# Layer 0's division and projection taken strip by strip, and attention scores with 64 keys at a time

## The chip, the cores and the metric

The kernel runs on one core of a Trainium2 chip. Its time is the device time of one execution in microseconds (us), the median of several runs. The core has five engines [...]: TensorE (PE, with its weight loads shown apart as PEld), VectorE (DVE), ScalarE (ACT), GpSimd (POOL) and SyncE (SP, which here issues DMA transfers). [...]

## The reference, cut to what matters

An image of 256 channels and 64 x 64 pixels goes through two layers. All numbers are fp32.

```python
# layer 0: linear attention over boxes, 8 heads of 32 channels
q, k = sigmoid(Wq @ x), sigmoid(Wk @ x)          # x after a group norm
v = v / norm(v)                                  # per head, v = Wv @ x
for w in (1, 2, 4):                              # boxes of 64, 32 and 16 pixels
    wk, wkv = box_sum(k), box_sum(k v^T)         # around each pixel
    attn = (q @ wkv) / (q @ wk + 1e-06)
    outs.append(attn)
x = x + Wout @ concat(outs) + bout
# layer 1: layer norm, softmax attention over 4096 tokens (8 heads of 32),
t = t + attention(layer_norm(t))
# then a mixture of 8 experts, two for each token
t = t + experts(layer_norm(t))
```

## The kernel before

**Order of pixels.** The image is cut into eight vertical strips `ix`, each 64 rows by 8 columns, 512 pixels. A strip has eight cells of 8 x 8 pixels. A block of 128 keys is two cells. `NB = 4` blocks make a strip.

**Layer 0, the two halves.** The outer loop `for g in range(KC)` does four heads at a time, 128 channels. For each half `prepare` projects keys, values and queries, makes sums over cells (`ssum`), and gets the denominators `den` of all three boxes and eight strips by matmuls into one PSUM bank. From it comes `rec`, 128 x 512: the row for strip `ix`, box `w` and head is `D * (ix % 4) + 4 * (NCH // 4 * w + ix // 4) + head`. Line 529 adds 1e-6, line 530 takes the reciprocal.

**Layer 0, the windows.** `attend` then goes through the three boxes, `for w in (2, 1, 0)`. A box reaches r = 1, 2 or 4 cells to each side (`REACH = (4, 2, 1)`). For r = 2 and r = 4 it first makes a vertical pass over four row bands `b` (L612 scores, L631 sums of whole cells, L643 values), copied into `raw` by ACT (L656), and then a pass over the strips `ix` (L681 scores, L697 values). For r = 1 there is the pass over strips alone. The result of a strip is added to `raw` by DVE (L707), or for r = 1 copied there by ACT (L709).

A *step* packs jobs of up to 512 queries. It has four score matmuls per job, one for each head, each with 32 rows of contraction; `masked` then multiplies each of the four heads' scores with a mask into `sm`. Heads 0 and 2 go by DVE from PSUM. Head 1, and in every other step head 3, are copied by ACT (L557) and multiplied by GpSimd (L561); head 3 else goes by DVE. The value matmuls of a step are put behind by two steps (`behind`, `tick`), so the order on TensorE is: scores of step n, values of step n - 2. Scores have six PSUM banks (`ps_sc`), sums have two (`ps_acc`).

**Layer 0, division and projection.** When a window is done, all steps in flight are flushed and two kinds of *chores* are listed. `division` takes two strips: a matmul (L721) with a constant of zeros and ones spreads the rows of `rec` over the 32 channels of each head, and DVE multiplies `raw` by it (L728). `projection` of a strip is eight 128 x 128 by 256 matmuls (L734), whose sums DVE adds to `t` (L738). `step_done` pops one chore after each step of the next window; the chores of the last window run at the end, with nothing beside them.

**Layer 1.** For each chunk of 512 queries `qc` and each half `g` there is a *group* of 32 steps, one for each block of 128 keys. A step has four score matmuls with 128 keys (L994) into two pairs of banks (`ps_two`, three pairs in all), two exponentials by ACT (L1004, one for each pair of heads), the value matmuls of the step before (L962), and sums of the exponentials by DVE in 30 of the 32 steps (L1011). The exponentials lie in a ring of four (`pe`). At the end of a group one matmul per head sums the last exponentials (`ps_den<-pe`), and a step later another adds the sums of DVE (`ps_den<-total`).

[...] 32 rows of contraction, and as many columns as it has keys or channels. In the profile 32*128 stands for 32 rows and 128 columns. Every fp32 matmul shows as two records.

Of the kernel before, what the change touches and what calls it, by code (L numbers as in the profile page):

```python
# [22 lines left out]
F32 = mybir.dt.float32  # L23
# [7 lines left out]
P = 128  # L31
C = 256
KC = C // P
N = 4096
NT = N // P
CH = 512
NCH = N // CH
IMG = 64
SW = 8
BH = 16  # L40
NB = IMG // BH
CELL = SW * SW
D = 32
GRP = 8
REACH = (4, 2, 1)
NW = len(REACH)
# [14 lines left out]
    "c": {"group": P, "xmask": 3 * SW, "ymask": SW * sum(_MCELLS), "ycut": 2 * SW},  # L61
    "k": {"sums": NCH // 4 * NW * D, "spread": NCH // 4 * NW * P, "before8": CH, "sides": NB * (SW + IMG + 1)},
    "m": {"rank": NE, "iota": P, "before": P, "ones": P, "number": 1, "high": 2 * NT, "spare": NU, "unit": NS + NE, "least": 2 * NE},
}
_AT, _W = {}, 0
# [6 lines left out]
def constants():  # L72
# [3 lines left out]
    out = np.zeros((P, _W), np.float32)  # L76
    p = np.arange(P)
# [9 lines left out]


    ns = range(NCH // 4 * NW)
    col = np.arange(D)[None, :]  # L90
    out[:, _AT["sums"]] = np.concatenate([col == 4 * n + p[:, None] // D for n in ns], 1)
    col = np.arange(P)[None, :]
    out[:, _AT["spread"]] = np.concatenate([p[:, None] % D == 4 * n + col // D for n in ns], 1)

# [20 lines left out]
def tile_conv_attn_hybrid(ctx: ExitStack, tc: tile.TileContext, a: dict, out: bass.AP):  # L115
    nc = tc.nc
# [26 lines left out]
    def tok(i):  # L143
        return slice(P * i, P * (i + 1))

    def chunk(i):
        return slice(CH * i, CH * (i + 1))
# [29 lines left out]
    def flush():  # L177
        while chains:
            tick()
# [9 lines left out]
    with ExitStack() as phase:  # L189
# [8 lines left out]

        big = phase.enter_context(tc.tile_pool(name="c_big", bufs=1))

        def weights(g):

            gs = slice(P * g, P * (g + 1))
            w3 = big.tile([P, KC, 3, P], F32, tag="w3", name="w3")
            for n, name in enumerate(("wqT", "wkT", "wvT")):
                nc.sync.dma_start(w3[:, :, n, :], a[name][:, gs].rearrange("(k p) o -> p k o", p=P))
            woT = big.tile([P, NW, C], F32, tag="woT", name="woT")
            nc.sync.dma_start(
                woT, a["woutT"].rearrange("(w g p) o -> p w g o", g=KC, p=P)[:, :, g, :]
            )  # L210
            return w3, woT

        with (
# [23 lines left out]
            for i in range(4):  # L237
                for k in range(KC):
                    at = slice(i * N // 4, (i + 1) * N // 4)
                    (nc.sync if k else nc.scalar).dma_start(x[:, k, at], xr[:, k, at])  # L240
            first = weights(0)
            ck = constants_of("k", wts)
# [63 lines left out]

        def prepare(g, prep, ps):


            bank, _ = banks(ps)  # L310
            two_banks = lambda: ps.tile([P, 2, CH], F32, tag="two", name="ps_two", bufs=3)
            w3, woT = weights(g) if g else first

# [215 lines left out]
            nc.vector.tensor_scalar_add(rec, den, 1e-6)  # L529
            nc.vector.reciprocal(rec, rec)  # L530
            return qk, v, ssum, rec, woT
# [3 lines left out]

        def finish(strip):

            while any(ix <= strip for ix, _ in chores):
                chores.pop(0)[1]()

        def step_done():
            tick()
            if chores:
                chores.pop(0)[1]()

        turns = [0]

        def masked(work, scs, used, pieces):


            turns[0] += 1
            sms = []
            for h, sc in enumerate(scs):
                sm = work.tile([P, CH], F32, tag="sm", name="sm", bufs=12)
                src, engine = sc, nc.vector
                if h == 1 or h == 3 and turns[0] % 2:
                    nc.scalar.copy(sm[:, :used], sc[:, :used])  # L557
                    src, engine = sm, nc.gpsimd
                for at, n, mk in pieces:
                    to, of = (z[:, at : at + n].rearrange("p (m n) -> p m n", n=mk.shape[-1]) for z in (sm, src))  # L560
                    engine.tensor_mul(to, of, mk.unsqueeze(1).to_broadcast(list(to.shape)))  # L561
                sms.append(sm)
            return sms
# [20 lines left out]
        def attend(g, work, ps, qk, v, ssum, rec, woT):  # L584
# [5 lines left out]
            raw = big.tile([P, NCH, CH], F32, tag="raw", name="raw")  # L590
            for w in (2, 1, 0):
                r = REACH[w]

                for b in (1, 2, 0, 3) if r > 1 else ():
# [8 lines left out]
                    for step in steps:  # L605
# [19 lines left out]
                        def use(places=places, sms=sms, accs=accs, begun=begun, b=b, last=step is steps[-1], raw=raw, r=r):  # L625
# [25 lines left out]
                            if last:  # L651

                                finish(NCH)
                                for u in range(2):
                                    q0 = P * b + CELL * u
                                    nc.scalar.copy(  # L656
                                        raw[:, :, q0 : q0 + CELL], accs[u].rearrange("p (i n) -> p i n", n=CELL)
                                    )
# [4 lines left out]
                for ix in range(NCH):  # L663
# [12 lines left out]
                    for step in steps:  # L676
                        scs = [score() for _ in range(4)]
                        at, places = 0, []
                        for n, i, c0, c1, *mk in step:
                            for h in range(4):  # L680
                                nc.tensor.matmul(  # L681
                                    scs[h][:, at : at + n],
                                    kT[hs[h], tok(i)],
                                    qT[hs[h], CH * ix + CELL * c0 : CH * ix + CELL * c1],
                                    start=True,
                                    stop=True,
                                    skip_group_check=True,
                                )
                            places.append((at, n, i, c0, c1, *mk))
                            at += n  # L690
                        sms = masked(work, scs, at, joined((p[0], p[1], *p[-2:]) for p in places))
                        step_done()

                        def use(places=places, sms=sms, acc=acc, begun=begun, ix=ix, last=step is steps[-1], raw=raw, r=r):
                            for at, n, i, c0, c1, *_ in places:
# [10 lines left out]
                            if last and r > 1:  # L706
                                nc.vector.tensor_add(raw[:, ix, :], acc, raw[:, ix, :])  # L707
                            elif last:
                                nc.scalar.copy(raw[:, ix, :], acc)  # L709

                        behind(lambda: None, use)

                flush()

                def division(ix, raw=raw, w=w):

                    for i, by in ((ix, score()), (ix + 1, score())):
                        at, n = slice(D * (i % 4), D * (i % 4 + 1)), NCH // 4 * w + i // 4  # L720
                        nc.tensor.matmul(  # L721
                            by,
                            ck["spread"][at, P * n : P * (n + 1)],
                            rec[at, :],
                            start=True,
                            stop=True,
                        )
                        nc.vector.tensor_mul(raw[:, i, :], raw[:, i, :], by)  # L728

                def projection(ix, raw=raw, w=w):  # L730
                    for b in range(0, NB, 2):
                        po = score().rearrange("p (i o) -> p i o", o=C)
                        for i in range(2):
                            nc.tensor.matmul(  # L734
                                po[:, i, :], raw[:, ix, tok(b + i)], woT[:, w, :], start=True, stop=True
                            )
                        to = t[:, NB * ix + b : NB * ix + b + 2, :C]
                        nc.vector.tensor_add(to, po, to)  # L738

                for ix in range(0, NCH + 2, 2):  # L740
                    if ix < NCH:
                        chores.append((ix, lambda ix=ix, f=division: f(ix)))
                    for i in (ix - 2, ix - 1) if ix else ():
                        chores.append((i, lambda i=i, f=projection: f(i)))
            finish(NCH)

        for g in range(KC):
            with tc.tile_pool(name="c_prep", bufs=1) as prep, psum("c_ps1", 2) as ps:
                of = prepare(g, prep, ps)
            with tc.tile_pool(name="c_work", bufs=1) as work, psum("c_ps2", 1) as ps:  # L750
                attend(g, work, ps, *of)
# [33 lines left out]
    with ExitStack() as phase:  # L785
# [163 lines left out]
        with tc.If(tame > 0) as branch:  # L949
            with (  # L950
# [33 lines left out]
                for qc in range(NCH):  # L984
                    for g in range(KC):
# [4 lines left out]
                        for i in range(NT):  # L990
                            sc = [two_banks() for _ in range(2)]
                            for hd in range(4):
                                hs = slice(D * hd, D * (hd + 1))
                                nc.tensor.matmul(  # L994
                                    sc[hd // 2][:, hd % 2, :],
                                    qk[hs, 1, g, tok(i)],
                                    qk[hs, 0, g, chunk(qc)],
                                    start=True,
                                    stop=True,
                                )  # L1000
                            pe = work.tile([P, 4, CH], F32, name="pe", bufs=4)
# [545 lines left out]
```

## Time and profile before

| | us |
|---|---|
| median of 3 runs | 2913.63 (2911.81 to 2914.61) |
| the profiled execution | 2911.62 |
| its span | 2909.8 |
| layer 0, half 0: windows | 141.6 to 526.2 |
| layer 0, half 1: windows | 642.1 to 1029.5 |
| layer 1: attention | 1147 to 2315 |
| layer 1: experts, output | 2315 to 2909.8 |

The profile is one execution. A matmul's record begins when it is issued and its end is modelled, so busy time of PE overlaps with its waits; the distance between the starts of two batches is what they really take. "Idle before" names what ended an engine's idle time. Times in the timeline are from the start of the span.

### The profile page before, as it was taken

The page shows a single profiled execution, that of the slowest core. Times are in us where ns is not written, and L with a number is a line of the kernel's source. Part 1 is how long each engine was busy: PE and PEld are TensorE (multiplying, and loading weights), DVE is VectorE, ACT ScalarE, POOL GpSimd, SP SyncE. Part 2 cuts the span into 40 slices and gives each one's busy share as a digit, 9 for nine tenths or more (in the row PEclk, how much of TensorE's full clock was granted, in tenths as well). Part 3 has the DMA queues.
Part 4 walks back from the last instruction along what each step waited for, and adds up shares of the span by engine and source line. Part 5 has one row for each costly group of instructions (what it writes and reads, how often), then busy time and mean ns, then how long its engine had stood idle before and what let it go on. Part 6 is the DMA issues. An engine that isn't in the chain of part 4 may idle for free. (4 is left out here: it accounts for less than half of the span.)

```text
span 2909.8 us, 62928 instructions
## 1 busy us (share of the span) xinstructions
PE 2769.2 (95%) x26286; PEld 1329.9 (46%) x26286; DVE 2082.3 (72%) x3009; ACT 1529.6 (53%) x2134; POOL 712.4 (24%) x808
## 2 busy tenths in 40 slices
PE   6899999989999988999999999999999969999996
PEld 5466442735644254222222222222222248888884
DVE  6776777577676886999999999999999941111113
ACT  3242323124233312888888888888888642222222
POOL 1085858109485711000000000000000012222220
PEclk9999999999999999999999999999999969999997
DMA  5000000000000000000000000000000056565665
GB/s 143 6 2 3 2 3 2 7 0 3 4 2 3 1 19 1 1 5 6 5 5 5 5 5 5 5 5 5 5 5 5 10 176 215 190 203 196 205 213 189
DMA packets 97546, 136.31 MB, mean 47 GB/s; under 512 B 18115, under 2 KB 79145, under 8 KB 97253
## 3 DMA queue, kind: packets, MB, share of 16 engines
q1 hardware_dynamic: 82360, 105.34, 11.2%
q0 software_dynamic: 6528, 17.83, 2.2%
q10 hardware_dynamic: 8364, 9.02, 0.9%
q8 instruction: 209, 3.42, 0.5%
q14 instruction: 85, 0.69, 0.1%
HBM read 114.57 MB, written 17.60 MB: 45 GB/s over the span
## 5 line engine op out<-in xcount | busy, mean ns | idle before, releaser
L1004 ACT ACTIVATE pe<-ps_two 128x1024 f32<-128x1024 f32 x1024 | 993.1, 1022 | 152.2 <-PE ps_two L994 146.9
L1011 DVE TENSOR_TENSOR total<-total,pe 128x1024 f32<-128x1024 f32 x928 | 1058.2, 1219 | 2.2 <-ACT pe L1004 2.2
L994 PE MATMUL ps_two<-qk 32*128 32x512 f32 x4096 | 630.6, 640 | 3.5 <-POOLq L949 1.8
L962 PE MATMUL ps_acc<-pe,v 128*32 128x512 f32 x4096 | 547.2, 605 | 0.1
L557 ACT COPY sm<-ps_sc 128x384 f32<-128x384 f32 (+4 forms) x486 | 232.5, 513 | 460.6 <-PE ps_sc L681 271.2
L561 POOL TENSOR_TENSOR sm<-sm,mask 128x192 f32<-128x192 f32 (+3 forms) x460 | 380.2, 860 | 232.7 <-ACT sm L557 232.5
L994 PEld LDWEIGHTS ps_two<-qk 32*128 32x128 f32 x4096 | 205.2, 183 | 419.5 <-PE ps_two L994 221.3
L561 DVE TENSOR_TENSOR sm<-ps_sc,mask 128x384 f32<-128x384 f32 (+3 forms) x708 | 324.1, 518 | 92.8 <-PE ps_sc L681 91.4
L1456 ACT ACTIVATE hid<-ps_hp,cols 128x256 f32<-128x256 f32 (+1 forms) x288 | 133.1, 462 | 360.4 <-PE ps_hp L1453 359.3
L1271 POOL MEMSET on<- 128x256 f32 x1 | 0.3, 311 | 1177.3 <-PE ps_den L962 1177.3
L962 PEld LDWEIGHTS ps_acc<-pe,v 128*32 128x32 f32 x4096 | 80.8, 108 | 390.3 <-issue 377.2
L681 PE MATMUL ps_sc<-qk 32*128 32x192 f32 (+3 forms) x2688 | 245.3, 446 | 5.7 <-DVE sm L561 2.9
L1453 PE MATMUL ps_hp<-xe,w 128*128 128x256 f32 (+1 forms) x1152 | 246.6, 370 | 0.0
L1462 PE MATMUL ps_yp<-w,hid 128*128 128x256 f32 x1088 | 240.8, 379 | 0.0
L1453 PEld LDWEIGHTS ps_hp<-xe,w 128*128 128x128 f32 x1152 | 201.1, 190 | 39.7 <-ACT hid L1456 5.6
L697 PE MATMUL ps_acc<-sm,v 128*32 128x192 f32 (+3 forms) x2688 | 216.6, 423 | 0.8 <-POOL sm L561 0.8
L1462 PEld LDWEIGHTS ps_yp<-w,hid 128*128 128x128 f32 x1088 | 204.2, 190 | 26.4
L1432 DVE TENSOR_SCALAR xe<-ps_tp,cols 128x256 f32<-128x256 f32 (+1 forms) x72 | 34.8, 525 | 239.3 <-PE ps_tp L1428 217.5
L561 POOL TENSOR_TENSOR sm<-sm,ycut 128x384 f32<-128x384 f32 (+4 forms) x150 | 150.8, 1024 | 140.9 <-ACT sm L557 140.6
L681 PEld LDWEIGHTS ps_sc<-qk 32*128 32x128 f32 x2688 | 126.3, 186 | 124.5 <-DVE sm L561 70.1
L561 DVE TENSOR_TENSOR sm<-ps_sc,ycut 128x512 f32<-128x512 f32 (+4 forms) x250 | 127.7, 562 | 65.2 <-PE ps_sc L612 63.2
L1464 DVE TENSOR_TENSOR y<-ps_yp,b 128x256 f32<-128x256 f32 x68 | 28.9, 425 | 195.1 <-PE ps_yp L1462 195.1
(239 smaller groups left out, 2244.3 us busy)
## 6 DMA issues: line engine op xcount, KB each, us to landing
w<-in_L_ffn_W SPq DMA_DIRECT2D x72, 1024.0 KB
b<-in_L_ffn_b SPq DMA_DIRECT2D x36, 128.0 KB
rows<-in_x SPq DMA_DIRECT2D x16, 256.0 KB
zrows<-act SPq DMA_DIRECT2D x4, 1024.0 KB
y<-yrows SPq DMA_DIRECT2D x8, 512.0 KB
y<-yrows ACTq DMA_DIRECT2D x8, 512.0 KB
rec<-recs SPq DMA_DIRECT2D x60, 64.0 KB
x<-in_x ACTq DMA_DIRECT2D x4, 512.0 KB
```

The lines of the kernel that those rows point to most:

```text
L557: nc.scalar.copy(sm[:, :used], sc[:, :used])
L561: engine.tensor_mul(to, of, mk.unsqueeze(1).to_broadcast(list(to.shape)))
L681: nc.tensor.matmul(scs[h][:, at : at + n], kT[hs[h], tok(i)], qT[hs[h], CH * ix + CELL * c0 : CH * ix + CELL * c1], start=True, stop=True, ...
L697: nc.tensor.matmul(acc[hs[h], CELL * c0 : CELL * c1], v[:, i, hs[h]], sms[h][:, at : at + n], start=not begun[0], stop=last and at == plac ...
L962: nc.tensor.matmul(to[D * hd : D * (hd + 1), :], lhsT(hd), rhs[:, hd, :], start=start, stop=stop, skip_group_check=True,)
L994: nc.tensor.matmul(sc[hd // 2][:, hd % 2, :], qk[hs, 1, g, tok(i)], qk[hs, 0, g, chunk(qc)], start=True, stop=True,)
L1004: nc.scalar.activation(pe[:, pair, :], s, AF.Exp, scale=C**-0.5)
L1011: add = nc.vector.tensor_add(to, first[:, pair, :] if i == 1 else to, pe[:, pair, :])
L1432: nc.vector.tensor_scalar(xe[:, k, :n], tp[:, k, :n], cols[:, gain], cols[:, shift], op0=ALU.mult, op1=ALU.add,)
L1453: nc.tensor.matmul(hp[:, :n], w1[:, k, tok(m)], x_now[:, k, :n], start=k == 0, stop=k == KC - 1)
L1456: nc.scalar.activation(hid[:, m, :n], hp[:, :n], AF.Gelu, bias=cols[:, m : m + 1])
L1462: nc.tensor.matmul(yp, hid[:, m, tok(j)], w2[:, m, :], start=m == 0, stop=m == NH - 1)
```

## The change

- **Reciprocals by transfers.** Line 530 goes. In `attend` the reciprocal of `rec` is taken in four pieces of 128 columns, as the first four chores; then `rec` is written to a DRAM tile `recs`, and for each strip and box a DMA reads four rows, each to 32 partitions, into `by` (ring of four, fetched four ahead). The constant `spread` and its matmuls go.
- **Each strip as soon as its sums are whole.** For r = 2 and r = 4 the last `use` of a strip lists a division on GpSimd, an empty chore and the projection. For r = 1 DVE multiplies the sums by `by` on their way from PSUM to `raw`, and the projection follows. There is no flush between windows. `owed` counts GpSimd's divisions: for each of them one step later keeps head 3 on DVE.
- **Smallest boxes last.** The order of w is (1, 0, 2), so r = 2, 4, 1.
- **64 keys at a time.** In the pass over strips a step that holds a single job makes two score matmuls with 64 keys each in place of one with 128; layer 1's attention does so in every step.
- `woT` is loaded by `weights_out` at the start of `prepare`; `w3` of the second half is loaded after the first `prepare`.

```diff
-            nc.vector.reciprocal(rec, rec)
             return qk, v, ssum, rec, woT
...
             turns[0] += 1
+            both = turns[0] % 2
+            if both and owed[0]:
+                both, owed[0] = 0, owed[0] - 1
...
-                if h == 1 or h == 3 and turns[0] % 2:
+                if h == 1 or h == 3 and both:
...
-            for w in (2, 1, 0):
+            recs = dram.tile([P, CH], F32, name="recs")
+            windows = (1, 0, 2)
+            order = [(w, ix) for w in windows for ix in range(NCH)]
+            held = []
+
+            def fetch():
+                if order:
+                    w, ix = order.pop(0)
+                    by = work.tile([P, CH], F32, name="by", bufs=4)
+                    row = D * (ix % 4) + 4 * (NCH // 4 * w + ix // 4)
+                    nc.sync.dma_start(by, recs[row : row + 4, :].unsqueeze(1).to_broadcast([4, D, CH]))
+                    held.append(by)
+
+            def turn_over():
+                nc.sync.dma_start(recs, rec)
+                for _ in range(4):
+                    fetch()
+
+            def reciprocal(z):
+                with tc.issue_after(latest[0]):
+                    nc.vector.reciprocal(z, z)
+
+            for i in range(4):
+                chores.append(lambda i=i: reciprocal(rec[:, tok(i)]))
+            chores.append(turn_over)
+            for w in windows:
                 r = REACH[w]
+                def division(ix, raw=raw):
+                    nc.gpsimd.tensor_mul(raw[:, ix, :], raw[:, ix, :], held.pop(0))
+                    owed[0] += 1
+                    fetch()
...
+                            rows = CELL if len(step) == 1 else P
                             for h in range(4):
-                                nc.tensor.matmul(
-                                    scs[h][:, at : at + n],
-                                    kT[hs[h], tok(i)],
+                                for u in range(0, P, rows):
+                                    nc.tensor.matmul(
+                                        scs[h][u : u + rows, at : at + n],
+                                        kT[hs[h], P * i + u : P * i + u + rows],
...
                             if last and r > 1:
                                 nc.vector.tensor_add(raw[:, ix, :], acc, raw[:, ix, :])
+                                chores.extend([lambda: division(ix), lambda: None, lambda: projection(ix)])
                             elif last:
-                                nc.scalar.copy(raw[:, ix, :], acc)
+                                if ix == 0:
+                                    finish()
+                                nc.vector.tensor_mul(raw[:, ix, :], acc, held.pop(0))
+                                fetch()
+                                chores.extend([lambda: None, lambda: projection(ix)])
...
-                flush()
-                def division(ix, raw=raw, w=w):
-                    for i, by in ((ix, score()), (ix + 1, score())):
-                        at, n = slice(D * (i % 4), D * (i % 4 + 1)), NCH // 4 * w + i // 4
-                        nc.tensor.matmul(by, ck["spread"][at, P * n : P * (n + 1)], rec[at, :], start=True, stop=True)
-                        nc.vector.tensor_mul(raw[:, i, :], raw[:, i, :], by)
...
-            finish(NCH)
+            flush()
+            finish()
...
-                                nc.tensor.matmul(
-                                    sc[hd // 2][:, hd % 2, :],
-                                    qk[hs, 1, g, tok(i)],
-                                    qk[hs, 0, g, chunk(qc)],
+                                for u in range(2):
+                                    nc.tensor.matmul(
+                                        sc[hd // 2][CELL * u : CELL * (u + 1), hd % 2, :],
+                                        qk[hs, 1, g, P * i + CELL * u : P * i + CELL * (u + 1)],
+                                        qk[hs, 0, g, chunk(qc)],
```

## The prediction

> **What bounds the kernel now.** I read the busy shares first, then windows by stage, then TensorE's own timeline in two stages. The page's busy times:
>
> ```profile
> PE 2769.2 (95%) x26286; PEld 1329.9 (46%) x26286; DVE 2082.3 (72%) x3009; ACT 1529.6 (53%) x2134; POOL 712.4 (24%) x808
> ```
>
> Three stretches, their columns length, then PE, PEld, DVE, ACT and POOL busy, TensorE's clock, DMA share, GB/s: most of layer 0's r = 1 stage, its r = 4 strips, and layer 1's attention.
>
> ```profile
> 141.60:228.00 86.40, 84.95 (x1364) 51.62 (x1368) 68.24 (x153) 35.46 (x73) 74.71 (x108) 0.96 0.01 2
> 434.00:507.00 73.00, 72.82 (x860) 20.24 (x852) 56.26 (x103) 29.53 (x61) 62.09 (x58) 1.00 0.01 2
> 1147.00:2315.00 1168.00, 1165.78 (x8560) 313.27 (x8560) 1128.07 (x1074) 1010.63 (x1056) 0.65 (x4) 1.00 0.02 5
> ```
>
> A busy PE can still be waiting, so I take the distance from the start of one batch of matmuls to the start of the next. In layer 0 (start, then modelled length):
>
> ```profile
> 436.70 1.01 PE L612 MATMUL ps_sc<-qk 32*64 32x448 f32 x16
> 437.64 0.77 PE L643 MATMUL ps_acc<-sm,v 64*32 64x320 f32 x16
> ...
> 440.12 0.90 PE L612 MATMUL ps_sc<-qk 32*64 32x384 f32 x16
> 440.95 0.98 PE L643 MATMUL ps_acc<-sm,v 64*32 64x448 f32 x16
> ...
> 444.92 0.93 PE L681 MATMUL ps_sc<-qk 32*128 32x384 f32 x8
> 445.78 0.77 PE L643 MATMUL ps_acc<-sm,v 64*32 64x320 f32 x16
> ...
> 449.89 1.14 PE L681 MATMUL ps_sc<-qk 32*128 32x512 f32 x8
> 450.96 0.85 PE L697 MATMUL ps_acc<-sm,v 128*32 128x384 f32 x8
> ```
>
> Equal batches repeat to 0.01 us, except for some waits of 0.04 to 0.2 us: TensorE is the bound of layer 0's window stages, so a matmul removed there is time saved. It also compares the two forms of score: 384 queries cost 0.83 us with 64 keys at a time (L612) and 0.86 us with 128 (L681).
>
> Layer 1's attention is closer. One step is a score batch and a value batch:
>
> ```profile
> 1500.60 1.22 PE L994 MATMUL ps_two<-qk 32*128 32x512 f32 x8
> 1501.74 1.06 PE L962 MATMUL ps_acc<-pe,v 128*32 128x512 f32 x8
> 1502.74 1.23 PE L994 MATMUL ps_two<-qk 32*128 32x512 f32 x8
> ```
>
> That is 1.14 + 1.00 us; over a group of 32 steps the mean is 2.15 us. VectorE adds two halves in 30 of the 32 steps, 1.135 us from start to start, so 2.27 us a step: it falls behind and catches up between groups. Its whole rest there is the 1.80 us in this view:
>
> ```profile
> 1505.71 5.77 DVE L1011 TENSOR_TENSOR total<-total,pe 128x1024 f32<-128x1024 f32 x5
> 1513.29 2.36 DVE L1011 TENSOR_TENSOR total<-pe 128x1024 f32<-128x1024 f32 x2 [1.80 <-ACT pe L1004]
> ```
>
> A group lasts 70.7 us (74.9 with the four projections of the previous chunk in it), so a faster TensorE can give at most 1.8 us a group here.
>
> [...] an fp32 matmul is two passes, and from the first pass to the second of the same head it is 533 ns at L994 (512 queries, 128 columns), 453 ns at L962 (32 columns) and 320 ns at L612 (320 queries, 64 columns). Taking off 427 or 267 ns for the queries leaves 106, 26 and 53. [...] the trace has 89 ns between the last query of one mode and the next mode's first matmul. [...] at 1525.91 layer 1 writes a small tile to DRAM and the load that depends on it is issued 1.4 us later[...].
>
> **The change, part by part.** Signs are changes of time on the path.
>
> 1. Spreading reciprocals by matmul goes. The 48 matmuls of L721 (96 records) take 26.9 us from their starts to the next batch's, all inside TensorE's queue: **-26.9**. In their place come two writes `recs<-rec` and 48 loads `by<-recs`, 256 KB each, on SyncE's queue. The loads run four strips ahead and a strip lasts at least 5 us, against 1.4 us plus an estimated 1 us for 256 KB (the 4 MB of x are in by 17 us, 1.06 us for each 256 KB): hidden. Next half's `w3` is ahead of them in SyncE's queue and `woT` behind, each needed only later.
>
> 2. The division. L728 (48 products, 0.68 us of DVE) becomes 32 products on GpSimd, priced by the nearest row, its 128x512 mask product of 1281 ns, and 16 on DVE that replace the 0.59 us ACT copies of L709. For each GpSimd division one head's mask product returns from GpSimd (1.0 to 1.28 us) to DVE (0.55 to 0.69). So GpSimd stays level, and DVE trades 32 x 0.68 for 32 x 0.6. The projection is queued two steps after the division, about 3.7 us of TensorE work, against about 1 us (DVE's sum) + 1.28. It could still wait where GpSimd is late, since it is 86% busy in the first stretch: 0 to 0.6 us for each of 32. I take **+2**, ends 0 and +19.
>
> 3. Projections now stand alone between steps. An isolated strip costs 1.92 us, 48 of them 92.2; today L734 takes 95.2, of which 5.9 is the wait for layer 1's biases, which stays, so 89.3: **+2.9**. The last strip of each half has an open DVE product, about 1 us each: **+2**. Their DVE sums (2 x 0.69) are what they were; the r = 1 stage, now last, gets them, and DVE rises there from 79% to about 83% (68.2 + 8 x 2.06 of 86.4 + 15.4 us).
>
> 4. The reciprocal of 3.35 us stands ahead of the first mask products: the first DVE product is at 144.73, just as it ends, and TensorE waits at the sixth score bank. Now it comes in four pieces of about 0.85 between steps of the r = 2 stage, where DVE needs 1.6 of about 1.9 us a step. Bounds 0 and -6.7 for the two halves: **-5**.
>
> 5. No flush between windows: the two value batches at 227.84 last 3.36 us against 2.79 without a wait, those at 366.73 2.62 against 1.78. Both halves: **-2.8**.
>
> 6. Scores of 64 keys in layer 0: 24 steps at r = 2 and 32 at r = 4 hold a single block, so 112 in all, each 27 ns shorter: **-3.0**.
>
> Layer 0 sums to **-31** (-26.9 + 2 + 2.9 + 2 - 5 - 2.8 - 3.0 = -30.8).
>
> 7. Scores of 64 keys in layer 1's attention, 512 steps. Now 16 records instead of 8. By L612's pattern (6.6 ns between records, 53 ns a load) a free batch shortens from 1.07 to 1.04 us. But it isn't free today: the second pair of heads waits for ScalarE to clear a score bank. From the start of a step to ScalarE's first exponential it is 1.174 us, 1.02 for that, 0.055 to the waiting matmul; from there 1.056 to the value batch and 0.995 for that. Two periods are 1.174 + 1.075 + 1.056 + 0.995 = 4.30, so 2.15, as measured. With 64 keys the first term becomes 1.134 and the third 1.016: 2.11. That is 32 x 0.043 = 1.4 us a group for TensorE. But then VectorE is 1.3 us later at the group's end, and `ps_den<-total` (L962) must wait for its last sum: today it starts 0.13 us after that. The next exponential comes 0.86 + 1.13 + 1.02 = 3.0 us after it, and VectorE has 2.27 us of sums until then: it still rests about 0.9 of the 1.80 us. Gain 0.9 by VectorE's account and 0.7 by TensorE's with a wait of 0.7; I take 0.8 x 16: **-13**, ends 0 and -29.
>
> Sum: -44. Against the profiled execution's own 2911.6 us that is 2868; the three runs shown have a median 2 us higher, so **2869**.
>
> **Rivals.**
> A. VectorE's rest disappears altogether, and the conv part gives its best (-7 in item 4, nothing in item 2): -29 - 35, about 2850. For it: the `pe` ring of four lets TensorE run ahead. Against: the wait at `ps_den` each group. 13%.
> B. GpSimd's divisions come late: +19 instead of +2, and attention gives only 5: about 2894. For it: 86% busy at r = 1, and at r = 2 the second 384-query score batch already waits 0.19 us for banks. Against: stages with divisions get 1.92 us more TensorE time for each, in which GpSimd catches up. 15%.
> C. Slower. The two key halves don't load beside each other in attention: a 53 ns load is exposed in each pass for the second half, for both pairs, 0.21 us a step, x 512 = +109: about 2990. It turns the sum from 0.06 us a step on (31 / 512). For it: twice the instructions at 512 queries, a shape that the trace doesn't hold. Against: L612 does just this at 448 in 0.94 us. 8%.
> D. The change doesn't do what it says, for instance layer 0 waits for the transfers: the first division is a whole r = 2 stage after the write, so 2%, and then near 2910.
>
> **How the numbers follow.** My case has 62%, with 2852 to 2886 from the bounds in items 2, 4 and 7. The range 2846 to 2896 takes in A and B. A measurement of this kernel tells 0.2% (6 us) from no change. Faster 0.89 (mine, A, B), same 0.03 (most of D and the edge of C), slower 0.08.
>
> **What would show it.** Right: no spreading matmul; score groups 32*64 with twice the count in attention; steps there near 2.11 us; the idle time before `total<-pe` about halved; `ps_den<-total` waiting for DVE; layer 0 ending about 31 us earlier, with its projections 1.92 us apart from the next batch. Wrong: projection matmuls idle on GpSimd's `raw` (B), attention steps above 2.15 us (C), DVE products waiting on `by` (D).

## The result, and the profile after

The changed kernel takes **2879.81 us** (median of 5 runs, 2876.29 to 2881.24) against 2913.63 for the kernel before (5 runs, 2910.74 to 2914.61): a ratio of 0.9886, 95% interval 0.9872 to 0.9899. Forecast were 2869 us, range 2846 to 2896. The profiled execution of after took 2876.29 us with a span of 2874.5 us, the shortest of its five; before's took 2911.62 with 2909.8.

From the page of after, the busy times and the row of the instruction queue (packets, MB, share of the DMA engines):

```profile
PE 2722.7 (95%) x31182; PEld 1265.9 (44%) x31182; DVE 2078.1 (72%) x3019; ACT 1504.6 (52%) x2086; POOL 717.9 (25%) x804
...
q8 instruction: 249, 4.08, 0.6%
```

The same row before:

```profile
q8 instruction: 209, 3.42, 0.5%
```

TensorE has less to do, 2722.7 for 2769.2 us, in 4,896 more matmul records, and the instruction queue moves 249 packets instead of 209. The windows of three stages after: the bands of r = 2, now first in the half; most of the r = 1 strips, now last; attention. Columns as before.

```profile
138.00:197.00 59.00, 47.71 (x1974) 33.76 (x1972) 30.12 (x50) 17.19 (x33) 31.46 (x27) 1.00 0.08 27
434.00:494.00 60.00, 60.00 (x898) 37.37 (x900) 49.53 (x109) 19.21 (x41) 47.62 (x69) 1.00 0.05 15
1120.00:2270.00 1150.00, 1148.17 (x12616) 274.41 (x12624) 1121.09 (x1069) 1006.15 (x1053) 0.00 (x0) 1.00 0.02 5
```

The r = 1 strips keep TensorE busy all of the time with their projections among them. In the first row something is wrong: TensorE is busy for 47.71 of 59 us, and no other engine is busier. No forecast spoke of that stage.

By stages, from TensorE's starts in the timeline (us):

| | before | after |
|---|---|---|
| half 0: `prepare` | 119.7 | 117.6 |
| half 0: windows | 384.6 | 374.0 |
| half 1: `prepare` | 116.0 | 115.4 |
| half 1: windows | 386.8 | 371.1 |
| last projection to layer 1's first score | 118.3 | 119.8 |
| attention, first to last score | 1161.1 | 1150.4 |
| to the first expert matmul | 66.9 | 69.1 |
| experts and output | 534.6 | 535.0 |

So 26.3 us come from the windows and about 9 from attention with the stretch after it (1228.0 to 1219.5); between executions with the same code for a stage these lengths differ by 3 to 4 us (attention with 64 keys 1150.3 to 1153.8 in the runs below, the windows of the changed kernel 742.2 to 746.0).

The timeline of after in the r = 4 strips:

```profile
358.92 1.13 PE L734 MATMUL ps_sc<-qk 32*64 32x512 f32 x16
359.98 0.85 PE L750 MATMUL ps_acc<-sm,v 128*32 128x384 f32 x8
360.76 1.99 PE L638 MATMUL ps_sc<-woT,raw 128*128 128x256 f32 x8
362.68 0.90 PE L734 MATMUL ps_sc<-qk 32*64 32x384 f32 x16
```

A single-block step has 16 score records with 64 columns, and the projection stands alone, 1.92 us to the next batch, as forecast. The answer for the tile `by` gives its transfers, the products that read it, why their engines were idle, and who waited for them:

```profile
L609 SPq DMA_DIRECT2D by<-recs x48: 507/507/726, 154.9 to 951.8; - x48
L630 POOL TENSOR_TENSOR raw<-raw,by x32: 1261/1277/1300, 208.7 to 902.2; 128x512 f32<-128x512 f32 x32
...
DVE raw L760: 7.5, 18
...
PEld ps_sc L638: 13.1, 26
PE ps_sc L638: 1.6, 2
```

GpSimd's products wait only for the sums (L760), none waits for a transfer. 26 weight loads of projections waited for a product, but only 2 matmuls did: the last strip of each half, whose product is DVE's. Rivals B and D did not happen.

In attention, two steps and VectorE's rest at the start of a group:

```profile
1490.78 1.17 PE L1025 MATMUL ps_two<-qk 32*64 32x512 f32 x16
1491.88 1.07 PE L991 MATMUL ps_acc<-pe,v 128*32 128x512 f32 x8
1492.88 1.22 PE L1025 MATMUL ps_two<-qk 32*64 32x512 f32 x16
1494.02 1.06 PE L991 MATMUL ps_acc<-pe,v 128*32 128x512 f32 x8
```

```profile
1481.34 2.36 DVE L1043 TENSOR_TENSOR total<-pe 128x1024 f32<-128x1024 f32 x2 [1.27 <-ACT pe L1036]
```

One step here takes 1.10 + 1.00, the other 1.14 + 1.00. A plain group goes from 70.72 to 70.23 us from start to start, the mean step without the `ps_den` batches from 2.153 to 2.138; VectorE keeps 1.27 of its 1.80 us of rest. Rival A (no rest) and rival C (steps above 2.15) are out.

**Where TensorE waits in the bands of r = 2.** Its waits there, from the first value batch to the last (engine, tile, line waited for; us, times, longest):

```profile
PE ps_acc L681 <- issue: 3.9, 3, 1.7
PE ps_sc L662 <- issue: 3.5, 5, 0.8
PE ps_acc L693 <- issue: 2.3, 5, 1.0
```

And a piece of its timeline (the count at the end of a line is of matmul records):

```profile
159.23 1.05 PE L693 MATMUL ps_acc<-sm,v 64*32 64x192 f32 x35
161.30 0.44 PE L693 MATMUL ps_acc<-sm,v 64*32 64x128 f32 x13 [1.02 <-issue]
161.68 1.12 PE L662 MATMUL ps_sc<-qk 32*64 32x192 f32 x48
162.73 1.19 PE L681 MATMUL ps_acc<-qk,ssum 32*32 32x64 f32 x67
165.58 1.09 PE L681 MATMUL ps_acc<-qk,ssum 32*32 32x64 f32 x61 [1.66 <-issue]
166.59 1.10 PE L693 MATMUL ps_acc<-sm,v 64*32 64x128 f32 x48
167.62 0.75 PE L662 MATMUL ps_sc<-qk 32*64 32x128 f32 x19
169.03 0.90 PE L662 MATMUL ps_sc<-qk 32*64 32x192 f32 x29 [0.66 <-issue]
```

"issue" means that no semaphore explains the wait, and the batches break in their middle: 35 records, a pause, 13 more; 67, a pause, 61. A job has 16 records, and the third job of a step reads and writes the same tiles as the first, so an operand can't be missing there. I formed two theories. **T1**: TensorE runs out of instructions. Each packet of the instruction queue is 16,384 bytes, and in this stage (half 0) one comes every 3.4 to 4.5 us. 15 packets start between 146.4 and 201.3 us, and the stage has 3,649 matmul and weight-load records, 243 to a packet. A cells batch (the 64 matmuls of L681 with the sums of whole cells: 128 records and 128 loads, about a packet by that count) takes 1.92 us when nothing holds it, half the time from one packet to the next. Before, the spreading and the projections of r = 1 stood in this stage; now it is first and nothing is left to project. **T2**: the score banks (the six places that hold TensorE's scores until other engines have read them), kept by VectorE's reciprocals and products, make the wait, and the label is wrong.

The trace decides much of this by itself. From the break at 161.30 to the one at 165.58 there are 13 + 48 + 67 = 128 matmul records, from there to the one at 169.03 again 61 + 48 + 19 = 128, each with its weight load: 256 records, and in each of the two stretches one packet ends. In the whole stage of half 0 TensorE's starts have 13 pauses longer than 0.46 us. All of them lie a whole multiple of 256 matmul and weight-load records apart, and each ends 1.2 to 1.6 us after a packet of the instruction queue has ended. From the first of them (149.02 us) to the last (198.86) 3,328 such records start and 13 packets end: 256 to a packet. The 12 pauses of half 1 do the same. Waits for banks or operands would have no reason to keep to that count.

The trace of before already had such breaks in its r = 2 bands, in the second part of them, where no projection was left to stand between the steps:

```profile
287.78 0.74 PE L631 MATMUL ps_acc<-qk,ssum 32*32 32x64 f32 x34 [0.91 <-issue]
298.42 0.74 PE L631 MATMUL ps_acc<-qk,ssum 32*32 32x64 f32 x34 [1.19 <-issue]
```

### The profile page after: what moved, and what is told of

It reads as the page before. It is cut to its first block, busy times and chain, and to the rows that moved or that the text cites. A ratio compares the mean times of both kernels' runs of the same rounds, so it can differ in the third digit from the quotient of the medians.

```text
span 2874.5 us, 73093 instructions
## 1 busy us (share of the span) xinstructions
PE 2722.7 (95%) x31182; PEld 1265.9 (44%) x31182; DVE 2078.1 (72%) x3019; ACT 1504.6 (52%) x2086; POOL 717.9 (25%) x804
## 4 chain that ended last, share of the span: by engine, by line
PE 57%; DMA 2%; DVE 1%; issue 1%; ACT 0%; SPq 0%; POOL 0%; ACTq 0%; DVEq 0%; POOLq 0%
PE ps_two L1025 20%; PE ps_acc L991 18%; PE ps_hp L1485 8%; PE ps_yp L1494 8%; PE ps_den L972 1%; PE ps_den L991 1%; DMA y<-yrows 1%; PE ps_tp L1460 1%; DMA w<-in_L_ffn_W 0%; PE ps_two L972 0%; DVE t L1537 0%; DMA yrows<-y,target 0%; DVE rec L1072 0%; ACT pe L1036 0%; DVE total L1043 0%
## 5 line engine op out<-in xcount | busy, mean ns | idle before, releaser
L1025 PE MATMUL ps_two<-qk 32*64 32x512 f32 x8192 | 620.2, 613 | 3.6 <-POOLq L978 1.8
L561 ACT COPY sm<-ps_sc 128x384 f32<-128x384 f32 (+3 forms) x454 | 218.5, 511 | 523.8 <-PE ps_sc L734 344.3
L565 DVE TENSOR_TENSOR sm<-ps_sc,mask 128x512 f32<-128x512 f32 (+3 forms) x740 | 340.0, 519 | 71.8 <-PE ps_sc L734 68.0
L565 POOL TENSOR_TENSOR sm<-sm,mask 128x192 f32<-128x192 f32 (+3 forms) x428 | 350.1, 847 | 111.9 <-ACT sm L561 111.5
L1025 PEld LDWEIGHTS ps_two<-qk 32*64 32x64 f32 x8192 | 166.5, 129 | 421.0 <-PE ps_two L1025 379.0
L734 PE MATMUL ps_sc<-qk 32*64 32x384 f32 (+3 forms) x3584 | 231.9, 458 | 0.0
L1485 PEld LDWEIGHTS ps_hp<-xe,w 128*128 128x128 f32 x1152 | 201.3, 190 | 39.5 <-ACT hid L1488 5.3
L750 PE MATMUL ps_acc<-sm,v 128*32 128x256 f32 (+3 forms) x2688 | 213.2, 419 | 0.2
L565 DVE TENSOR_TENSOR sm<-ps_sc,ycut 128x384 f32<-128x384 f32 (+4 forms) x254 | 128.8, 559 | 90.0 <-PE ps_sc L662 88.0
L734 PEld LDWEIGHTS ps_sc<-qk 32*64 32x64 f32 (+1 forms) x3584 | 108.6, 157 | 111.4 <-DVE sm L565 67.6
```

Source lines behind the costliest of these rows:

```text
L565: done = engine.tensor_mul(to, of, mk.unsqueeze(1).to_broadcast(list(to.shape)))
L734: nc.tensor.matmul(scs[h][u : u + rows, at : at + n], kT[hs[h], P * i + u : P * i + u + rows], qT[hs[h], CH * ix + CELL * c0 : CH * ix + C ...
L750: nc.tensor.matmul(acc[hs[h], CELL * c0 : CELL * c1], v[:, i, hs[h]], sms[h][:, at : at + n], start=not begun[0], stop=last and at == plac ...
L1025: nc.tensor.matmul(sc[hd // 2][CELL * u : CELL * (u + 1), hd % 2, :], qk[hs, 1, g, P * i + CELL * u : P * i + CELL * (u + 1)], qk[hs, 0, g ...
L1485: nc.tensor.matmul(hp[:, :n], w1[:, k, tok(m)], x_now[:, k, :n], start=k == 0, stop=k == KC - 1)
```

## The experiments

Times are compared with runs of the kernel before on the same chip; "the changed kernel" on that chip is taken as 0.9886 of it, which by the interval of that ratio is good to about 4 us.

**Which part gave what.** The kernel before with 64 keys at a time in attention alone:

```diff
-                                nc.tensor.matmul(sc[hd // 2][:, hd % 2, :], qk[hs, 1, g, tok(i)], ...)
+                                for u in range(2):
+                                    nc.tensor.matmul(
+                                        sc[hd // 2][CELL * u : CELL * (u + 1), hd % 2, :],
+                                        qk[hs, 1, g, P * i + CELL * u : P * i + CELL * (u + 1)], ...)
```

> The kernel before with one part of the change: 64 keys at a time in layer 1's attention, nothing else. If the parts are independent, the attention gives here what the two traces show between its first and last score, 1161.1 to 1150.4 us, less the 2.2 us that VectorE's backlog gives back after it: 8 to 11 us faster than the kernel before (about 2904). If the gain seen in the whole change came from elsewhere (another start of the stage, other instruction addresses), it is within 3 us of the kernel before. If the second key half's weight loads were exposed (rival C of the prediction), it is slower.

2899.19 us against 2910.1, ratio 0.996 (0.9946 to 0.9973): -10.9. (The 2.2 us that the expectation takes off for VectorE's backlog don't show: here the first expert matmul comes 66.1 us after the last score, where it came 66.9 after it in the kernel before.) And the opposite, the changed kernel with attention as it was:

> The changed kernel with 128 keys at a time in layer 1's attention: layer 0's part alone. By the sum of the traces (windows 384.6 to 374.0 and 386.8 to 371.1, preparation 2.4 less) it is 24 to 29 us faster than the kernel before (about 2887) and 8 to 11 slower than the changed kernel. If the parts interact, the two parts don't add to the 34 us of the whole change.

2888.11 us, ratio 0.992 (0.9906 to 0.9934): -22.0, a little less than the 24 to 29 expected. The two sum to -32.9, the whole change to -33.8: the parts don't disturb each other. Forecast were -13 and -31, so nearly all that is missing is missing in layer 0. (In the trace of this run layer 0's windows are 25.4 us shorter than before, but the stretch to the first expert matmul, whose code is the same, is 2.0 us longer.)

**Is TensorE's queue the bound of layer 0?** 48 dead matmuls in the form of the spreading ones, two ahead of every second projection:

```diff
+                def spread(ix):
+                    at = slice(D * (ix % 4), D * (ix % 4 + 1))
+                    nc.tensor.matmul(score(), kT[at, :P], qT[at, :CH], start=True, stop=True)
```

> The changed kernel with the 48 spreading matmuls put back as dead work (32 rows by 128 columns, 512 queries, two strips one after the other, into a score bank that nobody reads), before every second projection. If TensorE's queue bounds layer 0, they cost what L721 took, about 25 us (1.06 for each of 24 pairs): near 2905. If the stretches with projections have slack that waits for other engines, they cost less than 12.

2902.52 us, ratio 0.9972 (0.9961 to 0.9983): 25.6 us above the changed kernel, where the forecast had 26.9 for these matmuls. So the queue is the bound where projections stand. The r = 2 bands hold none of the dead matmuls and stay at 54.9 and 54.0 us, so of them this run says nothing.

**Are the waits in the bands free room?** Nine dead projections a half (16 records and loads, 1.92 us each, 34.6 us in all), one behind every second step of the r = 2 bands:

```diff
+            def filler():
+                for _ in range(2):
+                    po = score().rearrange("p (i o) -> p i o", o=C)
+                    for i in range(2):
+                        nc.tensor.matmul(po[:, i, :], v[:, i, :], woT[:, 0, :], start=True, stop=True)
```

> The changed kernel with dead projections (four 128x128 by 256 matmuls, 1.92 us of TensorE and 16 instruction records) after every second step of the r = 2 bands: 9 for each half, 34.6 us of TensorE work in all. Theory 1: the bands' waits (15 us over the sum of their shortest batches, for each half) are TensorE's wait for its own instructions, since these small matmuls use up 256 of them in about 3 us and a block of 256 arrives every 3.4 to 4.2 us; then most of the filler is free: 5 to 18 us slower. Theory 2: the waits come from score banks that VectorE frees late, the reciprocals among its work; then the filler, which takes two more banks, costs its full 30 to 35 us.

2891.39 us, ratio 0.9931 (0.9916 to 0.9946): 14.5 us above the changed kernel for 34.6 us of work. The bands grow from 54.9 and 54.0 us to 60.1 and 61.3. Their windows, of half 0, with the dead projections:

```profile
150.00:210.10 60.10, 56.37 (x1889) 41.65 (x1888) 26.09 (x46) 16.13 (x31) 28.57 (x27) 1.00 0.07 26
```

That says that the room was there, not what made it. So the same filling again, with as much TensorE time in the same two score banks, but 256 records in each: dead copies of the cells batch.

```diff
+            def filler(r, b):
+                two = [score(), score()]
+                for u, ix in ((u, ix) for u in range(2) for ix in range(NCH)):
+                    for h in range(4):
+                        q0 = P * b + CELL * u
+                        nc.tensor.matmul(
+                            two[u][hs[h], CELL * ix : CELL * (ix + 1)],
+                            ssum[r][hs[h], ix, 2 * b + u, :], qcells[hs[h], ix, q0 : q0 + CELL], ...)
```

> The changed kernel with 9 dead copies of a cells batch (64 matmuls of 32*32 with 64 queries, 256 records with their loads, 1.92 us of TensorE) in each half's r = 2 bands, in the places where the run with dead projections had 9 dead batches of 16 records and the same 1.92 us, into the same two score banks. T1 (TensorE waits in the r = 2 bands for its instructions, which come at about 67 records a us there): 9 x 256 / 67 = 34 us a half, so the value batches of the bands take about 55 + 34 = 89 us from first to last and the kernel about 2948. T2 (it waits for score banks, VectorE or GpSimd): the dead batches fill the same waits as the dead projections, +5 to +7 us a half, and the kernel is near that run's 2891.

2943.73 us, ratio 1.0118 (1.0101 to 1.0135): 67 us above the changed kernel, 52 above the other filling. The windows of the bands of half 0, here and in the changed kernel:

```profile
150.80:234.30 83.50, 66.59 (x2853) 50.01 (x2848) 25.73 (x46) 16.13 (x31) 28.11 (x26) 0.94 0.06 20
```

```profile
146.40:201.30 54.90, 45.27 (x1825) 31.41 (x1824) 26.00 (x46) 16.11 (x31) 29.22 (x28) 1.00 0.08 28
```

(2853 + 2848) / 83.5 = 68.3 records a us, and (1825 + 1824) / 54.9 = 66.5: with 56% more instructions the rate is the same, while the work of the other engines is what it was. A length that follows the number of instructions and not the TensorE work is T1. The expectation had 89 us for 83.5: an added batch cost 3.2 us of the stage (28.6 / 9), not 3.8. TensorE's clock was 0.94 in this stretch, which accounts for at most 5 of the 83.5 us. The pauses again lie multiples of 256 records apart, 19 of them in half 0 and 20 in half 1. So it is the supply of instructions that holds the bands; what sets the time from packet to packet was not tested.

**VectorE's reciprocals** as the cause, left out:

```diff
-                with tc.issue_after(latest[0]):
-                    nc.vector.reciprocal(z, z)
+                pass
```

> The changed kernel without the four reciprocal pieces (4 x 0.94 us of VectorE a half); the reciprocal itself is left out. T1: the r = 2 bands of each half stay at 54 to 55 us from the first to the last value batch, and the kernel is within 3 us of the changed one (2877 to 2883). T2 (VectorE's reciprocals hold the score banks): the bands are 3 us or more shorter in each half, 2874 or less.

2878.32 us, ratio 0.9892 (0.9876 to 0.9909); bands of 52.8 and 53.1 us. They are 2.1 and 0.9 us shorter, less than the 3 that T2 asked for, and the whole is no faster. In the last two runs below, with the reciprocals in place, the same bands take 53.1 to 53.7 us, so even this difference need not be the reciprocals'.

**Smallest boxes last**, undone:

```diff
-            windows = (1, 0, 2)
+            windows = (2, 1, 0)
```

> The changed kernel with its boxes in the order r = 1, 2, 4, which undoes the part 'smallest boxes last' alone. The first strips of r = 1 now need their reciprocals about ten steps after the start. T1: the bands of r = 2 still hold almost no projection (one or two left over from r = 1), so they keep some 9 us of waits a half; the r = 1 stage now opens the half and takes the reciprocal pieces. I expect 2880 to 2890, a loss of a few us at the start of each half for the transfers. Rival (the order is what paid for the reciprocal and the flush): at least 6 us slower than the changed kernel, 2886 or more, with waits on the transfers or on VectorE in the first strips.

2886.56 us, ratio 0.9923 (0.9906 to 0.9939): 10 us slower than the changed kernel. The bands keep their waits (52.8 and 54.3 us long, 6.0 and 8.2 us of "issue"). The time lies in both forecasts' ranges; the waits that the rival named are there. VectorE's waits and TensorE's in half 0:

```profile
DVE raw L765 <- DMA by<-recs: 4.0, 1, 4.0
```

```profile
PE ps_sc L638 <- DVE raw L765: 3.6, 1, 3.6
```

With r = 1 first the reciprocals are needed before they have been to DRAM and back; with r = 2 first they have a whole stage of time. At the end of a half the last projection now waits 2.2 us for GpSimd, where it waited 0.8 for VectorE. Over both halves projections wait 11.4 us in four places for the divided sums, where the changed kernel waits 1.6: 9.8 us more, about the whole loss.

**A version meant to be better.** Projections have few instructions for their time (8 matmul records and 8 loads in 1.92 us), the bands many (256 in the 1.92 us of a free cells batch). The eight of r = 4 are kept back for the first eight steps of the r = 2 bands:

```diff
-            windows = (1, 0, 2)
+            windows = (0, 1, 2)
...
+                                if r == 4:
+                                    chores.append(lambda: division(ix))
+                                    late.append(lambda: projection(ix))
+                                else:
                                     chores.extend([lambda: division(ix), lambda: None, lambda: projection(ix)])
```

and `step_done` takes one from `late`, when `chores` is empty and the window is r = 2.

> A version meant to be better: the order is r = 4, 2, 1, and the eight projections of r = 4 are kept back, one for each of the first eight steps of the r = 2 bands; its divisions stay where they were. T1: a projection costs 1.92 us of TensorE with 16 records, and in the r = 2 bands most of it falls into time in which instructions are waited for: by the run with dead projections 9 of them added 5.2 to 7.3 us a half, so 8 add about 5.6 where they took 15.4: 8 to 10 us a half saved, about 2862. T2: projections cost the same everywhere, within 3 us of the changed kernel. Risk: r = 4's strips now have less TensorE work for each GpSimd division, so a few us can be lost there.

**2865.17 us**, ratio 0.9846 (0.983 to 0.9863), 11 us faster than the changed kernel and the fastest of all. Its bands:

```profile
269.80:331.60 61.80, 56.64 (x1888) 41.20 (x1880) 34.59 (x59) 16.14 (x31) 28.13 (x26) 1.00 0.03 8
```

They take 61.8 and 60.1 us, 13 us more over both halves, for 30.7 us of projections taken in: 17.7 us gained there, as T1 says. The windows as a whole are only 12 us shorter than the changed kernel's (733.0 to 745.1), where 16 to 20 were expected. Part of the rest lies in r = 4's bands, which now open the half: their score batches take 58.0 us instead of 50.6, where opening with r = 2 had cost 3.6 in waits. The new order of windows was not run alone.

**Who sets the step in attention?** VectorE with fewer sums:

```diff
-                            elif i < NT - 1:
+                            elif i < NT - 1 and i % 4:
```

> The changed kernel with VectorE adding the exponentials in 23 of a group's 32 steps instead of 30 (the keys of steps 4, 8, ... 28 are left out of the denominators). TA (TensorE and ScalarE set the step): the attention's mean step stays at 2.13 to 2.14 us, the groups at 70.2 us and the stretch from the first to the last score at 1150 us within 4; only the 2.2 us more ahead of the first expert matmul goes back (69.1 to 67). TB (VectorE's backlog holds the steps by the four buffers of exponentials): the step falls to the predicted 2.11, so 0.8 us a group, and the stretch is 13 us shorter or more, kernel 2865 or less.

2876.58 us, ratio 0.9881 (0.9864 to 0.9897), plain groups of 70.43 us, 1154.6 from the first to the last score (1150.3 to 1153.8 in the other runs with 64 keys). VectorE's rest at a group's start becomes

```profile
1557.97 2.36 DVE L1043 TENSOR_TENSOR total<-pe 128x1024 f32<-128x1024 f32 x2 [5.65 <-ACT pe L1036]
```

and the steps are no shorter, the groups even 0.2 us longer: TA, not TB. The stretch to the first expert matmul falls to 63.8 us (66.1 to 69.4 in the other runs with 64 keys), further than expected.

**64 keys in layer 0's strips**, undone:

```diff
-                            rows = CELL if len(step) == 1 else P
+                            rows = P
```

> The changed kernel with 128 keys at a time in all strips of layer 0: undoes that part alone. By the prediction's price 112 steps x 27 ns: 3 us slower, 2880 to 2883. Rival (in TensorE's queue the shorter load also lets the score banks free earlier): 6 us or more.

2879.1 us, ratio 0.9889 (0.9872 to 0.9905): by the time alone it can't be told from the changed kernel. In the timeline the strips, from the first score of a window's strips to the last of the strips that follow without bands between, take 493.5 us in the four stretches where the changed kernel has 489.2. So the part shortens the strips by about 4 us. That it shortens the kernel is not shown: in this run the bands happened to be shorter, and its windows as a whole take 742.9 us against 745.1.

## Why the prediction was right, and where its sum was not

The sign, the order of the parts and the bound were right: layer 0's windows are TensorE's queue wherever projections stand (48 dead matmuls cost 25.6 us), and attention and layer 0 gave separately what they gave together. The step that failed is the reading that a window's time is the sum of its batches: in the bands of r = 2 it isn't. The forecast of 2869 lies 11 us under the result, and the sum shows most of where. That it came so near is partly luck: of the 13.3 us that the bands cost, the other terms of layer 0, together better than forecast, covered 9.0. Sizes below are start-to-start sums over TensorE's batches, both halves.

| item | forecast | found |
|---|---|---|
| 1 spreading gone | -26.9 | -26.9 (none left) |
| 2 GpSimd's divisions late | +2 | 0 |
| 3 projections alone; last product open | +2.9, +2 | +4.0 (89.3 to 93.3); +1.6, counted in item 5's batches |
| 4 reciprocals not ahead of the masks | -5 | -6.7 |
| 5 no flush | -2.8 | -2.8 (value batches of strips 202.6 to 199.8, the open products' 1.6 in them) |
| 6 64 keys in the strips | -3.0 | -3.0 |
| fewer waits in the scores of the strips | none | -4.4 |
| bands of r = 2 short of instructions | none | **+13.3** |
| 7 attention | -13 | -10.9 (alone) |

- **The missing term.** Cells batches went from 37.2 to 43.75 us, the bands' value batches from 86.6 to 92.7, their scores by 0.7 apart from the start of a half: +13.3. The prediction read off that equal batches repeat to 0.01 us and took TensorE's queue as a sum of batches. That was read in the r = 4 bands and the strips, while the r = 2 bands of the same trace had waits of 0.91 and 1.19 us (above). It didn't ask how many instructions a stage issues, and it moved the r = 2 bands to where no projection stands between their steps. Item 3 counted a projection at 1.92 us wherever it stands; in these bands it had covered such waits, so it had cost less.
- **Item 4** came out at its bound. Before, the first three score batches of a half took 7.14 and 6.73 us, now 4.76 each; with the first value batches, waits of 10.3 us have become 3.6.
- **Item 2** was too careful: no matmul waited for a product of GpSimd's.
- **The fewer waits in the strips** were in no item. In the r = 2 strips 11 score batches of 384 queries wait about 0.19 us, where 22 did. The run with 128 keys has 10 such waits, so the 64 keys are not what removed them; what did was not tested.
- **Items 1 to 6** sum to -26.5 us with the new terms, the open products counted once, and the windows measure -26.3.
- **Weight loads.** Items 6 and 7 rest on loads of 106, 53 and 26 ns, an estimate that the two traces bear out. With 512 queries the second pass of a head starts 533 ns after the first with 128 columns (L994 before), 480 with 64 (L1025 after) and 453 with 32 (L962 before): 0.83 ns a column. With 64 columns it is 320 ns at 320 queries (L612 before) and 480 at 512: 0.83 ns a query, which gives the 427 and 267 ns that the prediction takes off. From 128 to 64 columns the shortest score batches of 512 queries in attention went from 1.071 to 1.044 us, those of 384 in the strips from 0.857 to 0.830: the 27 ns of item 6.
- **Item 7.** Two things of the working were wrong. The time from a step's start to ScalarE's first exponential was to fall from 1.174 to 1.134 us. Over all steps its mean is 1.195, where it was 1.190; only the quickest steps fell, from 1.17 to 1.15, although the second pass of each head starts at 0.480 instead of 0.533. So the step fell to 2.138 and not to 2.11, and a plain group by 0.49 us instead of 0.8. Why ScalarE starts no earlier was not tested. And `ps_den<-total` does not wait for VectorE, except in one group of 15: the distance from the `ps_den<-pe` batch to it is 2.90 us, 2.92 before. The forecast had it start 0.13 us after VectorE's last sum. That is when its weight load starts; the matmul itself stood 0.54 to 0.84 us behind the sum in most groups, and stands 0.10 to 0.23 behind it now. With VectorE's rest at 5.65 us the group is no shorter, so VectorE's account was not in play.

## What to carry to other kernels

A queue that is full in one stage need not be full in the next (here TensorE was busy for 60 of 60 us in the r = 1 strips and for 47.71 of 59 in the r = 2 bands): before a stage is moved or its fillers are taken out, count the instructions that it issues per us, not only its TensorE time. Here it paid to put work with long instructions (the projections' 128 x 128 matmuls, 16 records and loads in 1.92 us) between batches of short ones: keeping back eight projections in each half, with the order of windows that this needs, was worth 11 us, at no work saved. When a wait is labelled "issue" and breaks a batch in its middle, count the instructions from one break to the next: here it was 256 or a multiple of it every time. Then fill the wait once with few and once with many instructions: the difference names the cause.

## What the runs showed of the hardware

In the r = 2 bands TensorE's instructions came in packets of 16 KB every 3.4 to 4.5 us, TensorE's pauses lay 256 of its records or a multiple of that apart and ended 1.2 to 1.6 us after a packet, and the two stages that were short of them (the changed kernel's and that with the dead cells batches) ran at 66.5 and 68.3 records and loads a us, although a single cells batch runs at 133 (256 in 1.92 us). Transfers beside it made no difference that can be seen: the median distance of two packets was 3.86 us with 28 GB/s moving (the changed kernel), 3.52 with 20 (dead cells batches), and 3.68 in the bands of the version meant to be better, with 8.
